# Edge lists in DRAM, read back in chunks, and other buffer depths in the edge-sum stage of a graph block

## Chip, cores and metric

The kernel runs on one core of a Trainium2 chip. The metric is the device time of one launch in microseconds (us), the median of three runs. The profile is of one further execution, with a span from its first to its last instruction.

## The reference

There are 6250 nodes with 256 features each and 200000 edges, sorted by target. In short:

```python
xn  = layernorm(x)
# graph part: weighted sum over neighbours, self loop included
deg = count of edges into a node + 1;  dinv = 1/sqrt(deg)
h   = xn @ gnn_W
g   = relu(segment_sum(h[src] * (dinv[src]*dinv[dst]), dst) + dinv^2*h + gnn_b)
# mixer: linear attention over all nodes, layer norm, two-layer MLP, layer norm
x   = x + g + mix(xn)
# feed-forward: each node goes to the best of 8 experts, capacity 977
x   = x + expert_ffn(layernorm(x))
```

## The kernel before

The nodes are 49 blocks of 128 (the last has 106). The program has three stages.

**Stage 1, to about 300 us.** It normalizes x, computes q, k and v, and searches the sorted list of targets for where each block begins (`search`). Scaled rows `xs = xn*dinv` go in two forms: as three bf16 parts in SBUF (`xs3`, 128 partitions x 49 blocks x 768) and as float32 pairs in DRAM (`g_dram`, 2 KB a row). `edge_lists` then writes four lists that stay in SBUF to the end of stage 2: `idx` and `rel` (for each of 816 tiles of 128 edges the source row and the target's place in its block) and `hiT` and `loT` (for each of 25 even blocks, 22 groups of 2 x 128 edges, the block and place of each source). At the end a flag is read; if the data does not fit the layout, a general path (`tc.If(flag == 1)`) computes the sums instead and empties the lists.

**Stage 2, about 302 to 1645 us.** It sums over the edges, in two ways, and does the rest of the graph part and of the mixer beside it. Three Python generators are interleaved by hand (`tc.manual_schedule`), so every engine has one fixed order:

- `gather`, for the 24 odd blocks, 34 tiles each, 816 in all. Step j starts the indirect DMA of 128 rows of `g_dram` into `gt` (L891, on POOL's queue), and builds a one-hot `oh` of the targets on DVE (L895). It then multiplies tile j - LAG: `ps += oh^T gt` (L906, 512 columns, in PSUM pool `gaps` with two banks). The first tile of a block is preceded by two matmuls with the identity (L903, L904) that add the self loop. The last is followed by `put_sum`: ACT copies one half of `ps` out (L825), DVE adds the other (L827). `GB` = 9 buffers hold `gt` and `oh`; `LAG` = 7.
- `dense`, for the 25 even blocks. A block takes 11 steps. A step builds four pairs of one-hots on DVE (`onehots`: `lo` 128 wide at L838, `hi` 294 wide at L840), multiplies the pairs of the step before (L874, four matmuls into two PSUM tiles `bp`, pool `bups` with two banks), and ACT casts both to a slice of the count matrix `A` (L875). Beside it, the matrix of the block before is multiplied with `xs3`: some 15 matmuls a step (L858) into `ps_d`, copied out by `put_sum`.
- `rounds`, 25 rounds of two blocks: the mixer for one pair, and for an earlier pair, whose sums are there, the graph weight, layer norm, gate, choice of expert, and an indirect DMA of its rows to `xbuf` (L984, also on POOL's queue).

The interleaving is set by counts: one step of `gather` in each pass of the loop, `dense` in proportion (286 steps on 823 passes, about one in three), and `SIDE` = 0.74 steps of `rounds`. PSUM's eight banks are spent as `mmps` 3 (for `rounds`), `gaps` 2, `deps` 1, `bups` 2.

**Stage 3, from about 1700 us.** The eight experts run one after the other from `xbuf`, and rows are scattered to the output.

Of the kernel before, what the change touches and what calls it, by code (L numbers as in the profile page):

```python
# [17 lines left out]
P = 128  # L18
N_NODES = 6250
N_EDGES = 200000  # L20
D = 256
# [22 lines left out]
EB = 34  # L44
NGT = NGB * EB
NGC = (NGT + P - 1) // P
GB = 9
LAG = 7
SIDE = 0.74
NX = 6  # L50
FIRST = 0.58
ROW = 2 * D + 2
# [10 lines left out]
def graph_block_kernel(  # L63
# [30 lines left out]
    g_dram = dram.tile([N_NODES, 2 * D], F32, name="g_dram")  # L94
    agg = dram.tile([AGR, D], F32, name="agg")
    deg_dram = dram.tile([AGR, 1], F32, name="deg_dram")
    q_dram = dram.tile([len(twos), P, 2, 2 * P], F32, name="q_dram")
    xbuf = dram.tile([SLOTS, ROW], F32, name="xbuf")

    main = ExitStack()  # L100
    lists = main.enter_context(tc.tile_pool(name="lists", bufs=1))
    idx = lists.tile([P, NGC * P], I32, name="idx")
    rel = lists.tile([P, NGC * P], F32, name="rel")
    hiT = lists.tile([P, NDC, 2, 5 * NG], F32, name="hiT")
    loT = lists.tile([P, NDC, 2, 5 * NG], F32, name="loT")
    big = main.enter_context(tc.tile_pool(name="big", bufs=1))
    xs3 = big.tile([P, NB, 3 * D], BF16, name="xs3")
    xv = xs3.bitcast(F32)
# [353 lines left out]
    def edge_lists():  # L462
# [55 lines left out]
        for c in range(NGC):  # L518
            if c % 4 == 0:
                et = [rps.tile([P, 512], F32, name="et_ps", tag="et_ps", bufs=2) for _ in range(2)]  # L520
            gd, gs = got.pop(c)
            gf, gf2 = gd.bitcast(F32), gs.bitcast(F32)
            V.tensor_scalar(gf, gd, nfirst[:, c:c + 1], None, op0=OP.subtract)
            V.tensor_copy(gf2, gs)
            yield
            for e, w in zip(et, (gf, gf2)):
                nc.tensor.transpose(e[:, c % 4 * P:(c % 4 + 1) * P], w, ident)
            ask(c + 2)
            yield
            if c % 4 == 3 or c == NGC - 1:  # L530
                for o, e in zip((rel, idx), et):
                    nc.scalar.copy(o[:, (c - c % 4) * P:(c + 1) * P], e[:, :(c % 4 + 1) * P])
                yield
        for c in range(NDC):
            wd, ws = got.pop(NGC + c)
# [14 lines left out]
            lf = hs.bitcast(F32)  # L550
            V.tensor_copy(lf[:W], ws[:W])
            yield
            for v, o in ((kf, hiT), (lf, loT)):
                et_ps = rps.tile([P, 512], F32, name="et_ps", tag="et_ps", bufs=2)
                for h in range(2):
                    nc.tensor.transpose(et_ps[:, h * W:(h + 1) * W], v[:W, h * P:(h + 1) * P], ident[:W, :W])
                nc.scalar.copy(o[:, c].rearrange("p h g -> p (h g)"), et_ps[:, :2 * W])
            ask(NGC + c + 2)
            yield
        V.scalar_tensor_tensor(vend[:W], first[:W], float(N_EDGES - 2 * P) - 0.5, vend[:W], op0=OP.is_lt, op1=OP.mult)  # L560
# [147 lines left out]
    with tc.If(flag == 1):  # L708
        with tc.tile_pool(name="gp", bufs=1, side="right") as gp:
# [91 lines left out]
            for t0, n in fours:  # L801
# [1 line left out]
                xs = slot4("xs").rearrange("p (t d) -> p t d", d=D)  # L803
                nc.sync.dma_start(xs[:r, :n, :], node_rows(agg, t0, n))
                all_of(in_parts(t0, n, xs))
            V.memset(rel, -1.0)
            V.memset(hiT, 400.0)
    early.close()


    with tc.tile_pool(name="ga", bufs=GB, side="right") as ga, \
            tc.tile_pool(name="de", bufs=2, side="right") as de, \
            tc.tile_pool(name="gaps", bufs=2, space=PSUM) as gps, \
            tc.tile_pool(name="deps", bufs=1, space=PSUM) as dps, \
            tc.tile_pool(name="bups", bufs=2, space=PSUM) as bps, \
            tc.manual_schedule():
        sums = {}
        there = set()
# [2 lines left out]
        def put_sum(t, ps):  # L821
            gi = t // 2
            if gi not in sums:
                sums[gi] = pair("G", 3, "ag")
            nc.scalar.copy(sums[gi][:, t % 2, :], ps[:, :D])  # L825
            if t % 2:
                V.tensor_tensor(sums[gi][:, 1, :], ps[:, D:], sums[gi][:, 1, :], op=OP.add)  # L827
            there.add(t)

        def onehots(u, p):  # L830

            c, b = divmod(u, 5)
            o = []
            for g in (2 * p, 2 * p + 1):
                for h in range(2):
                    col = b * NG + g
                    lo = de.tile([P, P], BF16, name="lo", tag="lo", bufs=8)
                    V.tensor_scalar(lo, rowb, loT[:, c, h, col:col + 1], None, op0=OP.is_equal)  # L838
                    hi = de.tile([P, NB * GN], BF16, name="hi", tag="hi", bufs=8)
                    V.tensor_scalar(hi, hib, hiT[:, c, h, col:col + 1], None, op0=OP.is_equal)  # L840
                    o.append((lo, hi))
            return o

        def dense():

            mats, made = {}, None
            acc_ps = None
            half = NG // 2
            for u in range(ND + 1):
                for p in range(half):  # L850
                    if u >= 1 and p >= 1:

                        A = mats[u - 1]
                        if p == 1:
                            acc_ps = dps.tile([P, D], F32, name="ps_d", tag="ps_d")
                        for hi in range((p - 1) * NB // (half - 1), p * NB // (half - 1)):
                            for h in range(3):
                                nc.tensor.matmul(acc_ps, A[:, hi, :], xs3[:, hi, h * D:(h + 1) * D],  # L858
                                                 start=(hi == 0 and h == 0), stop=(hi == NB - 1 and h == 2))
                    coming = None  # L860
                    if u < ND:
                        if p == 0:
                            mats[u] = de.tile([P, NB, P], BF16, name="A", tag="A")
                        coming = (u, p, onehots(u, p))
                    if made is not None:
                        uu, pp, oh = made
                        for i in range(2):
                            g = 2 * pp + i
                            w = GN if g < NG - 2 else 4
                            at = GN * g if g < NG - 1 else P - 4  # L870
                            bp = bps.tile([P, 512], F32, name="bp", tag="bp")
                            for h in range(2):
                                lo, hi = oh[2 * i + h]
                                nc.tensor.matmul(bp[:, :NB * GN], lo, hi, start=(h == 0), stop=(h == 1))  # L874
                            nc.scalar.copy(mats[uu][:, :, at:at + w],  # L875
                                           bp[:, :NB * GN].rearrange("p (s k) -> p s k", k=GN)[:, :, :w])
                        if pp == half - 1:

                            V.tensor_tensor(mats[uu][:, 2 * uu, :], mats[uu][:, 2 * uu, :], identb, op=OP.add)
                    made = coming  # L880
                    if u >= 1 and p == half - 1:
                        put_sum(2 * (u - 1), acc_ps)
                    yield

        def gather():
            tiles = {}
            ps = None
            for j in range(NGT + LAG):
                if j < NGT:
                    gt = ga.tile([P, 2 * D], FR, name="gt", tag="gt")  # L890
                    nc.gpsimd.indirect_dma_start(  # L891
                        out=gt, out_offset=None, in_=g_dram,
                        in_offset=bass.IndirectOffsetOnAxis(ap=idx[:, j:j + 1], axis=0))
                    oh = ga.tile([P, P], FR, name="oh", tag="oh")
                    V.tensor_scalar(oh, rowb, rel[:, j:j + 1], None, op0=OP.is_equal)  # L895
                    tiles[j] = (gt, oh)
                i = j - LAG
                if i >= 0:
                    k, e = divmod(i, EB)
                    t = 2 * k + 1  # L900
                    if e == 0:
                        ps = gps.tile([P, 2 * D], F32, name="ps", tag="ps")
                        nc.tensor.matmul(ps, identb, xs3[:, t, :2 * D], start=True, stop=False)  # L903
                        nc.tensor.matmul(ps[:, D:], identb, xs3[:, t, 2 * D:], start=False, stop=False)  # L904
                    gt, oh = tiles.pop(i)
                    nc.tensor.matmul(ps, oh, gt, start=False, stop=(e == EB - 1))  # L906
                    if e == EB - 1:
                        put_sum(t, ps)
                yield
# [266 lines left out]
                    lgt = None  # L1176

        G, Dn, S = gather(), dense(), rounds()
        n_dense = (ND + 1) * (NG // 2)
        done_d = done_s = 0  # L1180
        alive = {"g": True, "d": True, "s": True}

# [7 lines left out]
        j = 0  # L1190
        while any(alive.values()):
            step("g", G)
            while alive["d"] and done_d * (NGT + LAG) < n_dense * (j + 1):
                step("d", Dn)
                done_d += 1
            while alive["s"] and done_s < SIDE * (j + 1):
                step("s", S)
                done_s += 1
            j += 1
# [141 lines left out]
```

## Time and profile before

| what | value |
|---|---|
| runs | 2054.58, 2057.87, 2075.50 us; median 2057.87 |
| profiled execution, own time / span | 2051.43 / 2049.6 us |
| TensorE clock granted, mean | 0.905 |
| PE, DVE, ACT, POOL busy, whole span | 80%, 62%, 34%, 45% |
| stage 2, 302 to 1645 us: PE, DVE, ACT, POOL busy | 1097.3, 964.0, 407.8, 841.0 us of 1343 |
| stage 2: granted clock, share of DMA engines | 0.91, 0.70 |

PE stands for TensorE's matmuls, DVE for VectorE, ACT for ScalarE, POOL for GpSimd, SP for SyncE, which issues most plain DMAs. The busy time of PE counts modelled ends of pipelined matmuls. A wait is idle time of an engine, put down to what ended it.

### The profile page before, as it was taken

Reading aid. Unit: us, or ns where it says so; the run is one execution under the profiler, and the core shown is the slowest. Engines: PE = TensorE matmul, PEld = TensorE weight load, DVE = VectorE, ACT = ScalarE, POOL = GpSimd, SP = SyncE. Lnnn points to the kernel's source line nnn. Section 1 sums busy time; section 2 is a strip of 40 time slices with the busy share of each in tenths; the row PEclk is TensorE's granted clock in tenths of the full one; section 3 lists DMA queues with packets and bytes.
Section 4 is the critical chain, followed back from the end, with each engine's and each line's share of the span. In section 5 each row is a group of like instructions: output and inputs, shape, how many; then the busy total and the mean of one; then the engine's idle time right before and its main releaser. Section 6 shows DMA issues by size and latency. Waiting matters only on the chain. (4 is left out here: it accounts for less than half of the span.)

```text
span 2049.6 us, 28653 instructions
## 1 busy us (share of the span) xinstructions
PE 1648.4 (80%) x9171; PEld 1203.4 (59%) x9171; DVE 1275.3 (62%) x5337; ACT 700.4 (34%) x1627; POOL 924.3 (45%) x957
## 2 busy tenths in 40 slices
PE   5787866887888888887878787887878737999996
PEld 2454544666666666665656565665656525586774
DVE  5767657677767778686757677776867431232332
ACT  2657952233333333232323232332323112233332
POOL 1022006666666666656656666665665610011111
PEclk9888997999998989898989899898999958999998
DMA  7346767777776677767767676667676615414220
GB/s 214 100 133 196 253 182 194 181 183 196 184 187 173 182 182 189 194 161 193 187 180 180 183 181 169 171 185 183 171 179 170 172 35 188 174 49 146 99 96 19
DMA packets 211319, 337.83 MB, mean 165 GB/s; under 512 B 30047, under 2 KB 79002, under 8 KB 211018
## 3 DMA queue, kind: packets, MB, share of 16 engines
q0 software_dynamic: 125424, 232.93, 44.3%
q1 hardware_dynamic: 85434, 101.74, 15.5%
q8 instruction: 81, 1.33, 0.3%
q10 hardware_dynamic: 288, 1.08, 0.1%
q14 instruction: 92, 0.75, 0.1%
HBM read 278.29 MB, written 60.06 MB: 165 GB/s over the span
## 5 line engine op out<-in xcount | busy, mean ns | idle before, releaser
L891 POOL DMA_INDIRECT gt<-g_dram,idx x816 | 794.8, 974 | 576.1 <-issue 168.7
L858 PE MATMUL ps_d<-xs,A 128*128 128x256 bf16 x3675 | 489.4, 287 | 41.3 <-issue 37.5
L875 ACT CAST A<-bp 128x294 bf16<-128x294 f32 (+1 forms) x550 | 200.6, 401 | 832.8 <-PE bp L874 231.0
L858 PEld LDWEIGHTS <-A 128*128 128x128 bf16 x3675 | 355.5, 103 | 171.5 <-issue 112.9
L906 PE MATMUL ps<-gt,oh 128*128 128x512 f32 x816 | 335.1, 484 | 42.6 <-DMA gt<-g_dram,idx 32.3
L840 DVE TENSOR_SCALAR hi<-hib,hiT 128x294 bf16<-128x294 bf16 x1100 | 351.0, 323 | 1.1 <-issue 1.1
L874 PE MATMUL bp<-hi,lo 128*128 128x294 bf16 x1100 | 216.0, 305 | 120.2 <-ACT A L875 39.6
L838 DVE TENSOR_SCALAR lo<-rowb,loT 128x128 bf16<-128x128 bf16 x1100 | 269.9, 245 | 3.2 <-PE ps_d L858 1.2
L895 DVE TENSOR_SCALAR oh<-rowb,rel 128x128 fp32r<-128x128 bf16 x816 | 207.2, 288 | 76.2 <-remote 30.4
L874 PEld LDWEIGHTS <-lo 128*128 128x128 bf16 x1100 | 109.6, 102 | 180.9 <-issue 57.3
L906 PEld LDWEIGHTS ps<-gt,oh 128*128 128x128 f32 x816 | 153.3, 206 | 76.5 <-DMA gt<-g_dram,idx 37.4
L1285 POOL DMA_INDIRECT out<-rep,who x43 | 42.4, 986 | 314.7 <-DVE rep L1283 226.8
L1257 PE MATMUL hpf<-xet,w1e 128*128 128x512 f32 (+2 forms) x544 | 154.1, 441 | 8.7 <-ACTq L1297 3.5
L1267 PE MATMUL ypf<-w2e,hm 128*128 128x256 f32 (+1 forms) x688 | 151.3, 379 | 0.0
L1267 PEld LDWEIGHTS ypf<-w2e,hm 128*128 128x128 f32 (+1 forms) x688 | 128.9, 188 | 21.9 <-issue 3.1
L1257 PEld LDWEIGHTS hpf<-xet,w1e 128*128 128x128 f32 x544 | 86.5, 193 | 70.0 <-issue 62.9
L1269 DVE TENSOR_TENSOR y<-ypf,fb_s 128x256 f32<-128x256 f32 (+1 forms) x43 | 18.2, 423 | 138.8 <-PE ypf L1267 138.8
L662 PE MATMUL mm<-wqkv_s,xnt 128*128 128x512 f32 (+1 forms) x196 | 101.5, 644 | 0.0
L1259 ACT ACTIVATE hm<-hpf,fb_s 128x512 f32<-128x512 f32 (+2 forms) x136 | 70.9, 525 | 84.6 <-PE hpf L1257 81.2
L1051 DVE TENSOR_SCALAR z<-mm 128x8 f32<-128x8 f32 (+1 forms) x49 | 7.9, 162 | 138.6 <-remote 82.6
L984 POOL DMA_INDIRECT xbuf<-slot,put x49 | 51.8, 1058 | 74.5 <-issue 45.4
L1101 ACT ACTIVATE s<-s,nb,rs 128x256 f32<-128x256 f32 (+1 forms) x98 | 53.6, 599 | 47.3 <-DVE rs_sr L194 29.8
(289 smaller groups left out, 2034.1 us busy)
## 6 DMA issues: line engine op xcount, KB each, us to landing
gt<-g_dram,idx POOLq DMA_INDIRECT x816
g_dram<-two SPq DMA_DIRECT2D x24, 512.0 KB
xt<-in_x SPq DMA_DIRECT2D x42, 256.0 KB
xbuf<-zeros SPq DMA_DIRECT2D x26, 384.0 KB
xe<-xbuf SPq DMA_DIRECT2D x8, 1028.0 KB
w1e<-in_fw SPq DMA_DIRECT2D x8, 1024.0 KB
w2e<-in_fw SPq DMA_DIRECT2D x8, 1024.0 KB
xe<-xbuf SPq DMA_DIRECT2D x8, 771.0 KB
```

The source lines that it names most:

```text
L662: nc.tensor.matmul(kp[:r, :], xnt[:, c, i * r:i * r + r], wqkv_s[:, c, D:3 * D], start=(c == 0), stop=(c == 1))
L838: V.tensor_scalar(lo, rowb, loT[:, c, h, col:col + 1], None, op0=OP.is_equal)
L840: V.tensor_scalar(hi, hib, hiT[:, c, h, col:col + 1], None, op0=OP.is_equal)
L858: nc.tensor.matmul(acc_ps, A[:, hi, :], xs3[:, hi, h * D:(h + 1) * D], start=(hi == 0 and h == 0), stop=(hi == NB - 1 and h == 2))
L874: nc.tensor.matmul(bp[:, :NB * GN], lo, hi, start=(h == 0), stop=(h == 1))
L875: nc.scalar.copy(mats[uu][:, :, at:at + w], bp[:, :NB * GN].rearrange("p (s k) -> p s k", k=GN)[:, :, :w])
L891: nc.gpsimd.indirect_dma_start(out=gt, out_offset=None, in_=g_dram, in_offset=bass.IndirectOffsetOnAxis(ap=idx[:, j:j + 1], axis=0))
L895: V.tensor_scalar(oh, rowb, rel[:, j:j + 1], None, op0=OP.is_equal)
L906: nc.tensor.matmul(ps, oh, gt, start=False, stop=(e == EB - 1))
L1257: nc.tensor.matmul(hp[:, :nn], w1e[:, c, f * P:(f + 1) * P], xet[:, c, at:at + nn], start=(c == 0), stop=(c == 1))
L1259: nc.scalar.activation(hm[:, f, :nn], hp[:, :nn], AF.Relu, bias=fb1_s[:, e * 8 + f:e * 8 + f + 1])
L1267: nc.tensor.matmul(yp[:r, :], hm[:, f, (i - i0) * P:(i - i0) * P + r], w2e[:, f, :], start=(f == 0), stop=(f == DFF // P - 1))
```

## The change

1. The four lists are no longer SBUF tiles. In stage 1 ACT copies each piece into a staging tile `st` (two buffers), and an SP DMA stores it in DRAM (`idx_l`, `rel_l`, `hi_l`, `lo_l`): 4 stores for the first two lists, 10 for the others. In stage 2 `gather_lists(c)` reads 128 columns of `idx` and `rel`, `dense_lists(c)` 220 columns of `hiT` and `loT`, into a pool `chunks` with two buffers. Chunks 0 and 1 are read at the start of the stage, the others about half a chunk to more than a chunk ahead. The general path empties the lists in DRAM.
2. `dense` keeps the one-hots of two steps instead of one; `lo` and `hi` have 12 buffers instead of 8. The product with `xs3` and the casts follow two steps behind the one-hots.
3. `bups` has three banks instead of two, `gaps` one instead of two. Between two blocks `gather` now gives one pass of the loop to the others without doing anything itself.
4. `GB` is 11 instead of 9, `LAG` 9 instead of 7. `SIDE` is 0.72, since there are now 848 passes instead of 823.

The core of the diff:

```diff
-GB = 9
-LAG = 7
-SIDE = 0.74
+GB = 11
+LAG = 9
+SIDE = 0.72
...
-    idx = lists.tile([P, NGC * P], I32, name="idx")
-    rel = lists.tile([P, NGC * P], F32, name="rel")
-    hiT = lists.tile([P, NDC, 2, 5 * NG], F32, name="hiT")
-    loT = lists.tile([P, NDC, 2, 5 * NG], F32, name="loT")
+    idx_l = dram.tile([P, NGC * P], I32, name="idx_l")      # rel_l, hi_l, lo_l likewise
...
-                    nc.scalar.copy(o[:, (c - c % 4) * P:(c + 1) * P], e[:, :(c % 4 + 1) * P])
+                    st = rw.tile([P, 512], F32, name="st", tag="st")
+                    ...
+                    nc.scalar.copy(st, e[:, :(c % 4 + 1) * P])
+                    nc.sync.dma_start(o[:, (c - c % 4) * P:(c + 1) * P], st)
...
-            tc.tile_pool(name="gaps", bufs=2, space=PSUM) as gps, \
+            tc.tile_pool(name="gaps", bufs=1, space=PSUM) as gps, \
-            tc.tile_pool(name="bups", bufs=2, space=PSUM) as bps, \
+            tc.tile_pool(name="bups", bufs=3, space=PSUM) as bps, \
...
+        def part(name, source, dtype=F32):
+            t = chunks.tile([P, source.shape[-1]], dtype, name=name, tag=name)
+            nc.sync.dma_start(t, source)
+            return t
...
+        gather_lists(0)
+        dense_lists(0)
+        gather_lists(1)
+        dense_lists(1)
...
+            for n in range((ND + 1) * half + 2):
+                u, p = divmod(n, half)
+                if u < ND:
+                    ...
+                    made.append((u, p, onehots(u, p)))
+                m = n - 2
+                ...                 # product of block u-1, counts and casts of step m
...
                     if e == 0:
+                        if k:
+                            yield
                         ps = gps.tile([P, 2 * D], F32, name="ps", tag="ps")
```

## The prediction

> **What bounds the kernel now.** I began with the page's busy times by slices, to see where the change lands.
>
> ```profile
> PE   5787866887888888887878787887878737999996
> ...
> POOL 1022006666666666656656666665665610011111
> PEclk9888997999998989898989899898999958999998
> ```
>
> Slices 7 to 32 are the edge sums (stage 2): PE near eight tenths, POOL near six, a granted clock that flickers below full. In the last slices PE is at nine and the clock at full, so the low clock belongs to a PE that stops and starts. The first and last stages are hardly touched; the forecast is about stage 2. Its sum by engine:
>
> ```profile
> 302.00:1645.00 1343.00, 1097.28 (x6925) 827.60 (x6924) 964.02 (x4391) 407.76 (x970) 841.04 (x860) 0.91 0.70 181
> ```
>
> PE 82%, DVE 72%, ACT 30%, POOL 63%, DMA 70%: no engine is full. POOL is fuller than it looks:
>
> ```profile
> L891 POOL DMA_INDIRECT gt<-g_dram,idx x816 | 794.8, 974 | 576.1 <-issue 168.7
> ```
>
> In the timeline, gathers in a row start 1.24 to 1.28 us apart: 0.94 to 0.97 busy and a constant 0.30 between. 816 x (0.974 + 0.30) = 1040 us, and 49 scatters to xbuf of 1.058 + 0.30 add 67: POOL alone needs 1106 of the 1343 us. PE's 1097 holds cold time; DVE needs 964. Three engines of similar load, each in a fixed order, lose the rest to each other. So next I read what PE waits for in this stage:
>
> ```profile
> PE bp L874 <- ACT A L875: 39.6, 26, 3.3
> PE ps_d L858 <- issue: 37.5, 49, 2.2
> PE ps L906 <- DMA gt<-g_dram,idx: 32.3, 24, 2.7
> PE bp L874 <- DVE lo L838: 17.0, 12, 8.5
> PE bp L874 <- issue: 16.5, 26, 3.2
> PE bp L874 <- DVE hi L840: 14.7, 14, 2.1
> ```
>
> All PE waits there come to some 240 us: for the bp banks 40, for one-hots or for other DVE work queued in front of them about 52 (17.0 + 14.7 and twelve smaller rows), for gathers 32 and 10 more before L906 with no cause shown, for nothing shown elsewhere about 70, for the mixer's own chains the rest. The last view is the timeline at a change of gathered block:
>
> ```profile
> 858.23 0.39 PE L903 MATMUL ps<-xs,identb 128*128 128x512 bf16 x1
> ...
> 861.74 0.71 ACT L875 CAST A<-bp 128x294 bf16<-128x294 f32 x2 [5.93 <-remote]
> 862.07 0.94 POOL L891 DMA_INDIRECT gt<-g_dram,idx  x1 [1.61 <-remote]
> 862.19 1.14 PE L874 MATMUL bp<-hi,lo 128*128 128x294 bf16 x4 [2.99 <-ACT A L875]
> ...
> 862.59 0.41 ACT L825 COPY ag<-ps 128x256 f32<-128x256 f32 x1
> ...
> 863.03 0.42 DVE L827 TENSOR_TENSOR ag<-ps,ag 128x256 f32<-128x256 f32 x1 [4.06 <-ACT ag L825]
> ```
>
> Two things are to be seen. The next block's first matmul (L903) runs 5.2 us before the old bank is empty (863.45), which needs the second gaps bank. And ACT and POOL are let go together, long after the matmuls that they wait for are shown.
>
> **What the Trainium skill says.** "TensorE: Matmul & The Clock Gate", section on the HAM clock gate, says that an idle PE falls to half clock and is full again after about 3.4 us of sustained work. The trace agrees in kind: 0.97 busy goes with clock 1.00 in the last stage, 0.82 with 0.91 here. A mean of 0.91 between half and full means 18% of the time at half. "Perfetto Trace Analysis", section on TensorE instructions, says that a matmul's shown end is an estimate; so part of PE's "wait for ACT" may be work, and I discount it. "DMA: Bandwidth & Descriptors", anatomy of one DMA, gives about 2 us fixed per DMA, which I use for the first chunk reads. Gathers here take longer: those started at 304.64 and 305.96 let their matmuls go at 310.00 and 311.41, 5.4 us.
>
> **Part by part.** The sum is made against the profiled execution, 2051.4 us by its own time; the median of the runs shown, 2057.9, is 6.5 above it.
>
> *One-hots two steps ahead.* The same DVE instructions, 2200 of them, only earlier. DVE may still not run more than a step past PE (12 buffers hold three steps, as 8 held two), but PE may now run ahead of DVE by two steps before it stops. A step is 1343/286 = 4.7 us. The DVE rows are waits of 1 to 4 us (one of 8.5 at the start), so one more step covers nearly all; I keep the start and a few others, 14 us: -38. DVE's own stops for PE's results (113 us before z L1051 with "remote" and bp as releasers) are what fills this slack.
>
> *Three bp banks.* A step uses two. Before, the first bp of a step waits for the first cast of the step before; now that first bp finds a bank free and the second waits for the same cast. The gain per stop is one bp of two matmuls, 0.2 to 0.4 us, sometimes the whole of a short stop: 26 x 0.4 = -10. The 40 us do not go.
>
> *LAG 9, GB 11.* Gathers 9 ahead at 1.27 us each stand 11.4 us before use instead of 8.9, against 5.4 us of flight. The stops for gathers average 1.35 us and reach 2.7, and they follow the xbuf scatters: at 699.5 to 702.7 POOL stands still for a scatter's slot and then four scatters of 1.36 us alternate with gathers. Two more gathers in hand cover 2.5 us of each of these 12 places: of 42 us, -25. POOL must have had the time to run ahead; its waits for PE (141 us for L906 alone) say so.
>
> *Follow-on.* These are -73 together. With PE faster, POOL's 1.27 us per gather and the late releases (in 79 of 275 steps the cast is released by "remote" or by the later ps_d matmuls) become the next wait. I let a third come back there: -49. Fewer stops raise the granted clock; one point of 0.91 on 1097 us: -10 (0 to -30).
>
> *One gaps bank.* Now L903 waits for ACT's L825 and DVE's L827, and everything behind it on PE waits too: the counts, the dense product, the mixer. I measured in the timeline, at all 23 block changes, the end of L827 minus the start of L903: from -1.9 to 7.35 us, the positive ones 44.1 in sum. The added pass gives PE about 1.3 us of other work in between (1343/823 = 1.63 us a pass at PE's 82%); what stays above 1.3 sums to 24.1. The largest (7.35, 5.2, 5.1) lie where PE is stopping anyway, so some of it is not new: +20, between +5 and +44. Before this change this wait is absent; that is its full price.
>
> *Chunk reads.* 8 SP DMAs at the start, then 5 x 2 and 3 x 2 more, 64 gathers (105 us) or more than two blocks ahead; SP stands up to 62 us before an output store (L1089), but that store is earlier in the order, so the read is not late. The first idx chunk stands before the first gather and the first oh: DVE restarts at 299.94 after the flag, and a DMA needs 2 to 4 us after SP has passed it: +4 (2 to 8). The order behind SP's queue: the reads of xt and q for the first rounds, a few tenths of a us each, which have slack.
>
> *Stage 1.* ACT's copies are the same, 14 in number; 14 stores join SP's queue, each behind ACT's copy, with g_dram stores, xbuf blanks and xt loads behind them. xt is loaded three groups ahead. +2 (0 to 6). The freed list space costs nothing. The tail after 1645 is the same chain, with a two-gather shorter starve at its front, in the -25.
>
> Sum: -49 - 10 + 20 + 4 + 2 = -33, so 2018 for the profiled kind of execution; with the 6.5 us to the median, 2025. Rounded down a little, since PE's best stretches (19.4 of 20 us busy at full clock near 750 us) show how much room there is: 2022.
>
> **Rivals.** *More is freed.* If PE's stops feed each other through the clock, the -73 comes whole and the clock rises by three points: -73 - 30 + 26 = -77, about 1980; at most twice that, since POOL's 1106 and the stops that stay bound the stage near 1200. For it: windows with no scatter and no DVE burst run at clock 1.00. Against: the 79 late releases, which no buffer here removes.
>
> *Nothing moves.* PE's waits are partly not waits (modelled ends), and POOL with its 0.82 load sets the pace, as it does after each batch of scatters. Then -73 shrinks to -25, and the costs of 26 cancel it: about 2058.
>
> *Slower: the single gaps bank.* If the added pass carries no PE work (two passes of three have no dense step), each block change costs its measured gap, 44 us, and PE standing still there holds back the release of gathers too, so that POOL, at 1.27 us each, cannot catch up: 44 + 12 for POOL + 6 - 25 = +37, about 2095. It decides from a mean stop at L903 of about 3 us (23 x 3 = 69 against 73 gained, with the clock against the 6 of reads). Measured is 1.9 without any slack, so a doubling is needed.
>
> *The change does not do what it says* only in the banks: three banks for two tiles a step is half a step. That is in the -10.
>
> **How the numbers follow.** Forecast (2000 to 2037) 0.42; more is freed 0.18; nothing moves 0.18; the slow rival 0.22. A measurement of this kernel can tell about 1% from no change. Faster by over 1%: 0.60; within 1%: 0.18; slower: 0.22. Range: from 1955 (most of the second case) to 2092 (most of the last).
>
> **What would show it.** Right: the PE rows "bp <- DVE" fall from about 52 to under 20 us and "L906 <- DMA gt" under 20; a new row before L903 with ACT ag or DVE ag as its releaser, 10 to 30 us; "bp <- ACT A" still there; the granted clock in the stage at 0.92 or above; the first gather later by 2 to 8 us. Wrong: L903's row over 60 us, POOL back to back throughout with PE waiting for gt, or a longer first stage.

## The result, and the profile after

The changed kernel takes 2081.5 us (median of 16 runs, 2071.8 to 2089.2) beside 2058.1 us for the kernel before (16 runs): ratio 1.0115, 95% interval 1.0097 to 1.0134. It is slower by 23 us where 36 us faster was forecast. Later groups of runs fell on different chips, and these come in two kinds. On some the kernel before takes 2056 to 2068 us (kind S; the result above, and three more groups), on others 1878 us (kind F; two groups). Each ratio below is against runs of the kernel before in its own group; it can differ by up to 0.2% from the quotient of the two medians that stand beside it. On kind F the same change is *faster*, 0.9839 (0.9812 to 0.9867).

The profiled execution after took 2084.1 us, span 2082.3, clock 0.894 (before: 2051.4, 2049.6, 0.905). The same views as those shown of before; first the page's slices, and its row of the gathers:

```profile
PE   5787856778796978797878888887778746899996
...
POOL 1022016555665665655666666666566610111111
PEclk9799987999898988798999999898889867999998
...
L931 POOL DMA_INDIRECT gt<-g_dram,idx x816 | 794.6, 974 | 592.8 <-PE ps L948 167.5
```

Stage 2 now reaches to about 1680 us. The gathers cost POOL the same (974 ns each), but the first starts at 302.26 and the last at 1669.32, one in 1.677 us; before it was 302.10 to 1640.94, one in 1.643. 28 of the 33 us between the two profiled executions are there. The stage's sum by engine, over a window that holds all of it:

```profile
302.00:1680.00 1378.00, 1096.10 (x6929) 828.86 (x6929) 968.82 (x4398) 405.01 (x971) 840.66 (x860) 0.89 0.69 178
```

No engine does noticeably more than before (PE 1097, DVE 964, POOL 841): the stage has become longer by idle time. PE's waits in it, after:

```profile
PE ps_d L901 <- issue: 50.1, 69, 1.9
PE bp L912 <- ACT A L913: 40.7, 26, 7.7
PE ps L945 <- DVE ag L838: 31.6, 12, 7.6
PE mm L208 <- ACT ag L836: 24.8, 6, 6.9
PE ps L948 <- DMA gt<-g_dram,idx: 18.9, 13, 4.2
PE mm L1087 <- DMA q<-q_dram: 17.8, 1, 17.8
...
PE bp L912 <- DVE hi L874: 5.3, 4, 3.0
```

Four of the six signs that the prediction named are there: all of "bp <- DVE" fell from 47 to 13 us (the 52 of the prediction is all of PE's waits for DVE, 5 of them not at bp), the gathers' row from 32 to 19, the row of the single gaps bank (L945) appeared, with 32 just above the range, and "bp <- ACT" stayed at 41. Two are not: the clock in the stage is 0.89 and not 0.92, and the first gather is 0.16 us late and not 2 to 8. And the waits of the stage sum to 288 us, before to 240. I put the rows of both kernels together by what waits: bp for DVE -34, gathers for DMA -13, but the identity matmuls for DVE +36, the mixer's matmuls for ACT +32 (24 to 55), ps_d without a cause +13, the first rounds' matmul for its q +18. What was taken away at one matmul is paid, by these rows, at others.

The chunk reads show at the start of the stage. The first gather is only 0.16 us late, but xt and q of the first rounds now stand behind eight list reads on SP, which before had gone ahead of the branch at the end of stage 1:

```profile
299.35 0.37 SPq L843 DMA_DIRECT2D idx<-idx_l  x1
...
310.35 1.22 PE L1087 MATMUL mm<-kvb,q 128*128 128x132 f32 x4 [17.82 <-DMA q<-q_dram]
```

This matmul started at 302.83 before, and the first product of a gather at 305.58; now that is 314.07. The first list read started at 299.35 and let the first gather go at 302.26, 2.9 us later. (The 2 us that the prediction took for such a read are, in the section of the Trainium skill that it names, those of DMAs issued by GpSimd; these are SP's.)

Last, a stretch of the timeline in the middle of the stage, which turned out to be the most telling (PE's, ACT's and POOL's lines):

```profile
854.42 2.14 PE L901 MATMUL ps_d<-xs,A 128*128 128x256 bf16 x9
855.15 0.94 POOL L931 DMA_INDIRECT gt<-g_dram,idx  x1 [0.31 <-PE ps L948]
...
858.33 0.37 PE L901 MATMUL ps_d<-xs,A 128*128 128x256 bf16 x1 [1.77 <-issue]
...
859.76 0.37 PE L901 MATMUL ps_d<-xs,A 128*128 128x256 bf16 x1 [1.06 <-issue]
860.59 0.94 POOL L931 DMA_INDIRECT gt<-g_dram,idx  x1 [0.30 <-issue]
861.17 0.37 PE L901 MATMUL ps_d<-xs,A 128*128 128x256 bf16 x1 [1.03 <-issue]
863.27 0.37 PE L901 MATMUL ps_d<-xs,A 128*128 128x256 bf16 x1 [1.73 <-issue]
...
864.22 0.71 ACT L913 CAST A<-bp 128x294 bf16<-128x294 f32 x2 [16.78 <-remote]
864.37 1.19 PE L912 MATMUL bp<-hi,lo 128*128 128x294 bf16 x4
864.55 0.94 POOL L931 DMA_INDIRECT gt<-g_dram,idx  x1 [3.03 <-remote]
```

Dense matmuls, which have all their operands and elsewhere run 15 in 1.81 us, creep along one at a time, over a microsecond apart and without a semaphore to wait for, while POOL issues gathers one after the other; the count matmuls that ACT casts here had been shown at 849.37. Then POOL runs out of free buffers and stops (861.53), and three microseconds later everything is let go at once. The prediction had seen these late releases ("let go together, long after the matmuls that they wait for are shown") and given them a third of the gain.

### The profile page after: what moved, and what is told of

Its sections match the earlier page's. It is cut to its first block, busy times and chain, and to the rows that moved or that the text cites. A ratio compares the mean times of both kernels' runs of the same rounds, so it can differ in the third digit from the quotient of the medians.

```text
span 2082.3 us, 28761 instructions
## 1 busy us (share of the span) xinstructions
PE 1643.0 (79%) x9171; PEld 1203.0 (58%) x9171; DVE 1277.9 (61%) x5337; ACT 697.5 (33%) x1627; POOL 924.2 (44%) x957
## 3 DMA queue, kind: packets, MB, share of 16 engines
q0 software_dynamic: 125424, 232.93, 43.8%
## 5 line engine op out<-in xcount | busy, mean ns | idle before, releaser
L901 PE MATMUL ps_d<-xs,A 128*128 128x256 bf16 x3675 | 499.1, 289 | 52.9 <-issue 50.1
L948 PE MATMUL ps<-gt,oh 128*128 128x512 f32 x816 | 329.8, 479 | 26.8 <-DMA gt<-g_dram,idx 18.9
L912 PE MATMUL bp<-hi,lo 128*128 128x294 bf16 x1100 | 208.9, 307 | 72.0 <-ACT A L913 40.7
```

## The experiments

Theory A is the prediction's ledger: a relieved wait is time, less a third. Theory B: something else paces stage 2, and a relieved wait reappears elsewhere. In the first group A also says that the loss is the single gaps bank; B is called a rival there, and a theory C says that the loss is the late start of the stage.

### First group, kind S (before 2067.8 us): which part costs

**The change with the old banks**, and without the extra pass between two blocks.

```diff
-SIDE = 0.72
+SIDE = 0.74
-            tc.tile_pool(name="gaps", bufs=1, space=PSUM) as gps, \
+            tc.tile_pool(name="gaps", bufs=2, space=PSUM) as gps, \
-            tc.tile_pool(name="bups", bufs=3, space=PSUM) as bps, \
+            tc.tile_pool(name="bups", bufs=2, space=PSUM) as bps, \
-                        if k:
-                            yield
-        n_gather = NGT + LAG + NGB - 1
+        n_gather = NGT + LAG
```

> The changed kernel with the old split of PSUM banks: two for the gathered sums, two for the counts, no empty pass between blocks (825 passes, SIDE 0.74). Lists in DRAM, one-hots two steps ahead and LAG 9 stay. Theory A (the single gaps bank is the loss): the 32 us of PE waiting at L945 for DVE and the waits of the mixer's transposes that follow from it go, time 2040 to 2050. Rival B (DVE's lateness is only met at another place, since PE has one order): the waits come back at the counts or the mixer, time 2070 to 2085. Rival C (the late start of the stage is the loss): 2070 to 2080.

Measured: 2068.2 us, ratio 1.001 (0.9994 to 1.0025): the loss is gone, but the 2040 to 2050 that theory A expected are missed.

**Before, with only the bank swap** and its extra pass: the same edit the other way round, in the kernel before.

```diff
-            tc.tile_pool(name="gaps", bufs=2, space=PSUM) as gps, \
+            tc.tile_pool(name="gaps", bufs=1, space=PSUM) as gps, \
-            tc.tile_pool(name="bups", bufs=2, space=PSUM) as bps, \
+            tc.tile_pool(name="bups", bufs=3, space=PSUM) as bps, \
```

> The kernel before with only the banks moved: one for the gathered sums with an empty pass between blocks (848 passes counting as in the changed kernel, SIDE 0.72), three for the counts. Theory A: 2078 to 2100, a row of 25 to 45 us of PE waiting for DVE ag before the identity matmuls. Rivals B and C: within 8 us of 2058.

Measured: 2080.2 us, 1.0077 (1.0055 to 1.0098). PE's waits show where:

```profile
PE ps L905 <- DVE ag L827: 19.7, 8, 5.5
```

**Lists in DRAM alone**: the edit of the first run, and `dense` and the two depths as before.

```diff
-GB = 11
-LAG = 9
+GB = 9
+LAG = 7
-            mats, made = {}, []
+            mats, made = {}, None
...
-                    lo = de.tile([P, P], BF16, name="lo", tag="lo", bufs=12)
+                    lo = de.tile([P, P], BF16, name="lo", tag="lo", bufs=8)
```

> The kernel before with only the lists moved to DRAM and read back in chunks; banks 2 and 2, one step ahead, GB 9, LAG 7, SIDE 0.74. Theory C: eight list reads stand on SP's queue after the flag, ahead of the first reads of x and q, which before were issued ahead of the flag; the first matmul of the mixer comes some 9 us later and the whole is 2066 to 2074. Theory A: within 5 us of 2058.

Measured: 2069.4 us, 1.0004 (0.9989 to 1.002). The start is late here too: the first product of a gather comes at 316.13.

**The change with the first xt and q reads ahead of the branch** (they are what the first `next(S)` issues), and four list reads at the start instead of eight.

```diff
-        gather_lists(0)
-        dense_lists(0)
-        gather_lists(1)
-        dense_lists(1)
-            if b == 2 and p == 0 and c:
+            if b == 2 and p == 0:
-                    if w == P // 2 and c:
+                    if w == P // 2:
...
-        done_d = done_s = 0
+        next(S)
+        gather_lists(0)
+        dense_lists(0)
+        done_d, done_s = 0, 1
```

> The changed kernel with the first reads of x and q put ahead of the list reads in the order (and with that ahead of the flag), and chunk 1 of the lists read half a chunk later, so that four list reads instead of eight stand at the start. Theory C: 8 to 12 us less than the changed kernel, about 2071. Theory A: same as the changed kernel to 5 us, or the gain is taken up later by the waits in the stage.

Measured: 2099.2 us, 1.0155 (1.0138 to 1.0172). The first product of a gather came at 310.12 instead of 314.07, and the whole, each against the kernel before in its own group, became 0.4% (some 8 us) slower than the change instead of faster. Why is open: the edit also moves a step of `rounds` and the later list reads in the order. Theory C has no support from it.

What follows: the swap of banks costs 0.77% (16 us, between 11 and 20) alone and 1.05% (22 us) inside the change, which is all of the loss; given the noise the two prices can't be told apart. It was run as a whole, with its extra pass and its `SIDE`; neither these nor the third bp bank were run by themselves. The lists in DRAM cost nothing that can be measured, late start included. And the two parts that were to bring 63 us bring nothing: 1.001 with them, 1.0004 without.

### Second group, same chip as the first (before 2068.0): the two parts by themselves, and what sets the pace

**One-hots two ahead only**, with lists in DRAM, old banks, LAG 7, GB 9. Against the lists alone:

```diff
-            mats, made = {}, None
+            mats, made = {}, []
...
-                    lo = de.tile([P, P], BF16, name="lo", tag="lo", bufs=8)
+                    lo = de.tile([P, P], BF16, name="lo", tag="lo", bufs=12)
```

> Edit lists in DRAM as after, banks of before (two for gathered sums, two for counts), 7 gathers ahead as before, and of the change only the one-hots built two steps ahead. The same without the two-ahead measured 1.0004 of before. Theory A (the prediction's): a stop of PE for a one-hot is lost time, so -38 us, a third given back: ratio 0.985 to 0.99. Theory B (PE's one order: a stop that goes reappears at the next matmul, because another engine sets the pace): 0.997 to 1.003, with bp<-DVE down from 63 us to under 30 and the total of PE's waits unchanged.

Measured: 2067.2 us, 1.0007 (0.9986 to 1.0028). "bp <- DVE" is 22 us in its trace against 63 without the edit, the sum of PE's waits 271 against 279.

**LAG 9 and GB 11 only**, with lists in DRAM and old banks, one-hots one ahead. Against the lists alone:

```diff
-GB = 9
-LAG = 7
+GB = 11
+LAG = 9
```

> Lists in DRAM and the banks of before, one-hots one step ahead, and of the change only LAG 9 and GB 11 (two more gathers in flight). Theory A: -25 us less a third, ratio about 0.992. Theory B: 0.997 to 1.003. A third possibility is a loss: every block's sum is complete two passes later in PE's order while the mixer's rounds keep their place, 1.003 to 1.008.

Measured: 2068.6 us, 1.0018 (1.0 to 1.0035). PE's row of waits for gathers is 8 us in its trace against 21 without the edit.

**Half the gathers**, in the change with the old banks:

```diff
-                    gt = ga.tile([P, 2 * D], FR, name="gt", tag="gt")
-                    nc.gpsimd.indirect_dma_start(
+                    if j % 2 == 0:
+                        gt = ga.tile([P, 2 * D], FR, name="gt", tag="gt")
+                        nc.gpsimd.indirect_dma_start(
```

> After with the banks of before, and only every second tile's rows gathered: the odd tile's matmul reads the rows of the tile before it, so half of the computation's gathered rows are left out. PE, ACT and DVE do the same work; POOL loses 408 gathers of 1.27 us (518 of its 1106 us) and the DMA half its bytes. If POOL's issue or the gathers' landing sets the pace of the stage (a form of the rival 'nothing moves'), the time falls by 60 us or more, ratio under 0.97. If PE's order with the late releases of ACT and DVE sets it, the fall is 25 us at most (the waits for gt), ratio 0.985 to 1.0.

Measured: 1826.0 us, 0.8827 (0.8793 to 0.8861): 242 us less, though PE waited for gathers only 22 us by its own row in the kernel with all of them. ACT's waits for the counts, first with all gathers and old banks (first run of the first group), then with half:

```profile
ACT A L913 <- remote: 342.5, 59, 18.0
ACT A L913 <- PE bp L912: 206.5, 119, 7.3
ACT A L913 <- PE ps L946: 146.3, 76, 9.6
ACT A L913 <- PE ps_d L901: 111.0, 23, 7.7
```

```profile
ACT A L913 <- PE bp L912: 427.5, 196, 9.3
...
ACT A L913 <- PE ps L947: 72.7, 36, 6.4
ACT A L913 <- remote: 54.3, 11, 11.1
```

The late releases ("remote", where the matmul that was waited for had long been shown) go with the gathers, 342 to 54 us. POOL's instructions and the bytes are not all that changes in this run: 11 buffers of `gt` now hold the rows for 22 tiles, so POOL may run much further ahead of PE.

**Half the wide one-hots**:

```diff
-                    hi = de.tile([P, NB * GN], BF16, name="hi", tag="hi", bufs=12)
-                    V.tensor_scalar(hi, hib, hiT[:, col:col + 1], None, op0=OP.is_equal)
+                    if h == 0:
+                        hi = de.tile([P, NB * GN], BF16, name="hi", tag="hi", bufs=12)
+                        V.tensor_scalar(hi, hib, hiT[:, col:col + 1], None, op0=OP.is_equal)
```

> After with the banks of before, and the second wide one-hot of each count left out: its matmul uses the first one's, so the counts are not those of the second half. PE, ACT and POOL do the same work; DVE loses 550 instructions of 0.32 us, 176 of 970 us in the stage. If DVE's load sets the pace (directly, or because the mixer's steps, the block sums' additions and the gather one-hots stand behind the one-hots in its queue), ratio 0.97 or less. If not, 0.99 to 1.0.

Measured: 2062.5 us, 0.9973 (0.9956 to 0.999). DVE with 176 us less work moves the time by 5.5: it does not set the pace.

What follows: theory B holds on this chip. Either part does to its own row what was forecast and nothing to the time that can be told from noise.

### Third group, a chip of kind F (before 1877.6 us): bytes, coupling, PE

**Half of each row** (1 KB), in the change with the old banks:

```diff
-                    gt = ga.tile([P, 2 * D], FR, name="gt", tag="gt")
+                    gt = ga.tile([P, D], FR, name="gt", tag="gt")
-                        out=gt, out_offset=None, in_=g_dram,
+                        out=gt, out_offset=None, in_=g_dram.rearrange("n (c d) -> (n c) d", c=2),
-                    nc.tensor.matmul(ps, oh, gt, start=False, stop=(e == EB - 1))
+                    nc.tensor.matmul(ps.rearrange("p (c d) -> p c d", c=2), oh,
+                                     gt.unsqueeze(1).to_broadcast([P, 2, D]), start=False, stop=(e == EB - 1))
```

> After with the banks of before, and every gather fetches only the first half of each row (1 KB instead of 2 KB): the matmul reads that half twice, so the second half of each gathered row is left out. POOL issues the same 816 gathers of 128 rows, PE, DVE and ACT do the same work; only the bytes are halved. Leaving out every second gather brought 242 us. If that came from POOL's issue (1.27 us a gather, 1106 us of the stage), this run changes little: ratio 0.98 to 1.0. If it came from the bytes that the DMA engines move, it brings most of the 242 us: ratio under 0.93.

Measured: 1837.2 us, 0.9795 (0.9765 to 0.9825). POOL's row in the groups of instructions (busy us, mean ns of one, then idle before them and what ended it) is what it is with whole rows on such a chip (987 ns in the next group):

```profile
L931 POOL DMA_INDIRECT gt<-g_dram,idx x816 | 801.9, 983 | 369.1 <-issue 123.1 <-DMA rel<-rel_l 116.5 <-PE ps L946 59.3
```

**GB 11 with LAG 7** in the change with the old banks:

```diff
-LAG = 9
+LAG = 7
```

> After with the banks of before and LAG 7 in place of 9, GB stays 11. In the kernel before and in the change GB minus LAG is 2: a gather and its one-hot need the buffer of the matmul that the order puts two passes earlier, so POOL and VectorE can't get more than two passes ahead of PE. Here it is four. If this coupling is what loses the time that no engine needs (stage 1343 us against POOL 1106 and PE 1097), ratio 0.96 to 0.985. If the gathers' own rate or landing is the limit, 0.995 to 1.005, and PE waits for gt again.

Measured: 1869.3 us, 0.9964 (0.9948 to 0.9981).

**Two of the three parts of the dense product**, in the change with the old banks:

```diff
-                        for h in range(3):
+                        for h in range(2):
...
-                                             start=(hi == 0 and h == 0), stop=(hi == NB - 1 and h == 2))
+                                             start=(hi == 0 and h == 0), stop=(hi == NB - 1 and h == 1))
```

> After with the banks of before, and the dense product with two of its three parts (h = 2 is left out): PE loses 1225 matmuls of 0.13 us at full clock, about 160 us of its 1088 busy us as profiled; POOL, DVE, ACT and the gathers stay. If PE's own order and load set the pace, ratio 0.93 to 0.95. If the gathers set it, 0.985 to 1.0, and PE's stops grow by what its work shrinks.

Measured: 1838.0 us, 0.9814 (0.9783 to 0.9845). PE had 1225 matmuls less to do, yet between 302 and 1470 us its busy time fell by 86 us only, from 1027.7 (the same kernel with all three parts, next group) to 942.1, as its clock fell from 0.94 to 0.91. Its row of waits for gathers, 65 us with all three parts, says where the rest went:

```profile
PE ps L946 <- DMA gt<-g_dram,idx: 133.6, 140, 3.4
```

What these three mean shows only beside the change itself on such a chip, in the next group.

### Fourth group, another chip of kind F (before 1878.3 us): the change there

Four kernels from above: the change unaltered, the change with the old banks, that with half rows, and that with LAG 7.

> The changed kernel unaltered, beside the kernel before on the chip of this group. The group before this one ran on a chip where the kernel before takes 1877.6 us instead of 2058 to 2068, with POOL issuing nearly without a pause. If the loss comes from the gaps bank alone, it is there on either kind of chip: 1.007 to 1.015 on a slow one; on a fast one, where PE waits for gathers anyway, part of each stop at a block change is absorbed by gathers that land meanwhile: 1.002 to 1.012. If the more gathers in flight pay where gathers are the limit, after is at or below 1.0 on a fast chip.

The change: 1849.3 us, 0.9839 (0.9812 to 0.9867).

> After with the banks of before (two for gathered sums, two for counts). On a slow chip it repeats 1.001. On a fast one: 0.99 to 1.0 if two more gathers in flight or the earlier one-hots pay there, 1.0 to 1.005 if they don't. Its distance from the unaltered change in the same group is the price of the bank swap: 1.0 per cent on the slow chip; the same on the fast one if it is PE's standing still that costs, less if gathers set the pace.

With the old banks: 1845.9 us, 0.9824 (0.9795 to 0.9854).

> Half of each gathered row left out (1 KB instead of 2 KB, read twice by the matmul), all else as after with the banks of before. On the fast chip 0.9795 of before. If this group's chip is slow: leaving out every second gather brought a ratio of 0.883 there. If the bytes are what that chip is slow in, under 0.93; if it is the number of gathers (POOL's instructions and what each of them makes the other engines wait for), 0.98 to 1.0.

Half rows: 1835.5 us, 0.9771 (0.9734 to 0.9807).

> GB 11 with LAG 7, banks of before, one-hots two ahead, lists in DRAM. On the fast chip 0.9964 of before. On a slow one, if the distance of two passes between a buffer's release and its next gather is what loses time there: 0.97 to 0.99; if not, 0.998 to 1.003. Beside the run with LAG 9 in the same group it shows what the two passes are worth.

LAG 7 instead of 9: 1869.3 us, 0.9946 (0.9928 to 0.9965).

So on kind F the change brings 29 us, by its medians: 23 of them from LAG 9 instead of 7, 9 from the lists, the earlier one-hots and GB 11 together, and -3 from the bank swap, which can't be told from nothing there. PE's waits in the unaltered change on this chip, to the stage's end at about 1460 us:

```profile
PE ps L948 <- DMA gt<-g_dram,idx: 55.4, 62, 3.1
PE mm L208 <- ACT s L1143: 24.2, 24, 5.6
PE ps L945 <- DVE ag L838: 19.9, 10, 5.9
PE mm L1087 <- DMA q<-q_dram: 17.2, 1, 17.2
```

then the page's slices of the same run, and the first row of ACT's waits:

```profile
PE   4787884898898989898989898998998459999996
...
POOL 0104003777777777776777777777777201101111
PEclk9888997899999999998999999999999779999998
```

```profile
ACT A L913 <- PE bp L912: 604.5, 235, 7.7
```

ACT waits only for counts that are really not there; no "remote" row is left, no ps_d without a cause. POOL stands at seven tenths instead of six, PE's clock at nine. The first and last gather start at 304.55 and 1440.49: one in 1.394 us; with the old banks 305.77 and 1434.17, 1128 us for what POOL alone needs 1106 for by the prediction's sum. By these figures POOL's issue is the pace here; the run that would test it, half of the gathers, is missing on kind F. That also reads the third group: PE's 1225 matmuls (0.9814 without them, 0.9824 with) are worth next to nothing, half of the bytes about 10 us (1835.5 against 1845.9), hardly more than the noise.

The wait at L945 is still 20 us, but half of it replaces waits for gathers: their row is 55 us here and 65 with the old banks, and the sum of all PE's waits in the stage is 143.7 us in both.

What LAG 9 removes is not mainly the wait for gathers. With LAG 7 the row is 64 us, with LAG 9 65; but with LAG 7 PE also waits at the same matmul behind other work of DVE:

```profile
PE ps L946 <- DMA gt<-g_dram,idx: 63.9, 56, 4.2
...
PE ps L946 <- DVE hi L874: 14.6, 10, 3.6
PE ps L946 <- DVE lo L872: 6.8, 7, 2.0
```

All such rows together are 34 us with LAG 7 and 2.4 with LAG 9: a gather's one-hot `oh` stands in DVE's queue in the pass of its gather, so two more passes are two more passes for DVE to be late in. That is read from the rows; no run moved the one-hot alone. GB minus LAG, four here and two in the kernel before, is worth at most the 9 us above: as the coupling that loses the stage's idle time it was to bring 1.5 to 4%.

### Fifth group, a third chip, kind S (before 2056.3 us)

**LAG 9 and GB 11 with one-hots one ahead** (the second group's kernel):

> Lists in DRAM, the banks of before, one-hots one step ahead, LAG 9 and GB 11. On the slow chip 1.0018. On a fast one, the same with one-hots two ahead is 0.9824, and with LAG 7 and two ahead 0.9946. If the two more gathers ahead are the whole gain there, as PE's only large wait is for gathers: 0.98 to 0.986. If the one-hots two ahead give what the prediction gave them (38 us, a third handed back): 0.992 to 1.0.

Measured: 2051.6 us, 0.9986 (0.9969 to 1.0003).

**One more of each**:

```diff
-GB = 11
-LAG = 9
+GB = 12
+LAG = 10
```

> The same with one more: LAG 10 and GB 12, which the one-step one-hots leave room for. If gathers that wait for use are what a fast chip lacks, a further 3 to 10 us below the run with LAG 9: 0.977 to 0.983 there, and the fastest of all that compute the whole; if POOL's issue of 1.25 us a gather is already reached, the same as LAG 9 within 0.003. On a slow chip 0.998 to 1.004.

Measured: 2067.2 us, 1.0054 (1.0034 to 1.0074).

**Half the gathers**:

> Every second gather left out (the odd tiles' matmuls read the rows of the tile before). On the slow chip this took 1826 us, 242 less than before there. If what makes the slow chip slow is tied to the gathers (about 190 us for 816 of them), a fast chip runs this kernel in nearly the same time, 1800 to 1840 us: ratio 0.96 to 0.98. If the chips differ in something else, it keeps its distance of 190 us: about 1640 us, ratio 0.87 to 0.89.

Measured: 1814.7 us, 0.882 (0.8789 to 0.8852).

On kind S, then, two more gathers in flight gain at most a fraction of a per cent, and a third one loses 0.7% against them, for a reason that is open; the 242 us that half of the gathers cost repeat on a second chip of the kind (241.6). Whether the one-hots two ahead matter on kind F was to be seen here and was not, since the chip was of the other kind; and the half of the gathers on kind F was not run.

No version beat both kernels on both kinds. The change with the old banks comes nearest: 1.001 and 0.9824.

## Why the prediction was wrong

| step | forecast, us | kind S | kind F |
|---|---|---|---|
| one-hots two ahead | -38 | 0 (1.0004 to 1.0007) | at most -9, with lists and GB 11 |
| LAG 9, GB 11 | -25 | +4 and -3 (1.0018, 0.9986), not told from 0 | -23 (LAG alone) |
| three bp banks and one gaps bank | -10 and +20 | +16 to +22 | +3, not told from 0 |
| lists: reads and stage 1 | +6 | 0 (1.0004) | in the -9 |
| a third comes back | +24 | all of it comes back | - |
| clock | -10 | lower than before (0.894 against 0.905) | - |
| sum, measured whole | -33 | +23 | -29 |

**The step that failed** is "Follow-on: I let a third come back there". On chips of kind S, as that of the result, all of the 63 us of the one-hots and gathers came back: the ratios are 1.0007 and 1.0018 with one of the two and 1.001 with both, beside 1.0004 with neither. The prediction had read the right sign for it, the late releases, and then gave "a third" without a working. The runs show what it is worth: the waits at bp and at the gathers did fall as counted, and the mixer's waits for ACT and the causeless ps_d took their place. The rival "nothing moves" had this part right, though not its reason: POOL did not issue steadily. It stopped again and again for buffers that PE had to free, and took 1.64 us a gather against 1.27.

**The bank swap** is the second. Its bounds (+5 to +44) held, its value did not: +20 for the gaps bank less 10 for the third bp bank was to leave +10, and 16 to 22 was measured, 36 us of wait at the identity matmuls. What the third bp bank is worth was not measured: all of "bp <- ACT" fell from 44 to 36 us with the swap alone, about the 10 that the prediction counted, but a fallen row was not time in the other two parts either. The slow rival had the place and the mechanism, a single gaps bank that holds up everything behind L945; its other half, that POOL can't catch up, fits the 1.677 us a gather but was not tested. Its sign of a stop of 3 us at every change did not come: 13 stops, 36 us in all, are 1.5 us over the 23 changes.

**Chunk reads.** The prediction said that xt and q "have slack". They had none: PE's first attention product stands 17.8 us for q. The price at the end of the kernel was nevertheless nothing, +4 forecast; the lists-only run shows it.

**The clock** in the stage was to rise from 0.91 to 0.92 and fell to 0.89, with PE busy for 1096 of 1378 us (80%) instead of 82%. On kind F it is 0.95 in the stage, with PE busy for 1023 of 1158 us (88%). So the traces agree in kind with what the prediction took from the section on the HAM clock gate of "TensorE: Matmul & The Clock Gate" in the Trainium skill, that an idle PE falls to half clock (their clock records hold only full and half); the direction of PE's idle time is what the prediction had wrong.

**LAG** came out at 23 of the 25 us on kind F, which is luck: the forecast was made from the waits of a chip of kind S, where it brings nothing, and the rows of kind F point to VectorE's one-hot and not to the gather's flight. The 5.4 us of flight were also a long case: the very first gather before let its product start after 3.5 us (302.10 to 305.58), and where the trace of the change on kind F lets a gather be followed to its landing (510 of 816) the median is 3.8 us.

What stays open: why PE's news comes late on kind S, and whether it is the news or PE's matmuls themselves that are late. That it is tied to the gathers is shown (342 to 54 us of "remote" with half of them, on one chip; 63 us in all ACT's rows on another); whether to POOL's issuing, to the transfers or to the buffers of `gt` is not, since the half rows and the LAG 7 with more buffers ran on kind F only.

## What to carry to other kernels

Before a wait is credited with its length, look for rows in which an engine is let go late with no cause that the profile can name: while such rows hold a stage, buffers and look-ahead only move the waits, and a run that halves the suspect's work tells more than the sum of the rows. A bank that the end of one accumulation and the start of the next share can cost its drain at every change: 16 to 22 us for 23 changes where PE waits little for gathers (19 us), nothing that can be told where it waits for them anyway (55 us). One chip's ratio is one chip's: this change is 1.2% slower on one kind and 1.6% faster on another.

## What the runs showed of the hardware

- The same kernel takes 2056 to 2068 us on chips of kind S and 1878 on two others, 9% less, with the same work, the same 1.24 to 1.25 us from gather to gather where POOL runs freely, and the same gather row (974 to 989 ns).
- One difference in the trace is how PE's completions are recorded. Between 400 and 1500 us the trace's records of the semaphore that PE counts up number 1647 in the profile after of the result, and 755 of them follow another within 60 ns, mostly at 34 ns; 68 silences are over 4 us. In the change on kind F, 2082 are recorded, none closer than 60 ns, and 7 silences are over 4 us. With half the gathers on kind S it is 235 of 1961, and 24. "Perfetto Trace Analysis" of the Trainium skill, section on TensorE instructions, says that a matmul's shown end is an estimate, and its summary of the profiler's windows that the passing on of its semaphore is not in them; the silences may be what this hides.
- The records themselves differ too. In the same stretch of the profile after, 1827 of PE's instructions count a semaphore up and 1647 counts are recorded; of DVE's 2604 only 1369 are, of ACT's 760 only 446. On kind F hardly one is missing (2082 of 2084, 3006 of 3006, 860 of 860). So a wait on kind S that the profile puts down to nothing ("issue") can be one whose record is missing; a "remote" row rests on a record that is there.
- The transfers are not slower on kind S. In the change the packets of POOL's queue filled 43.8% of the 16 DMA engines' 2082.3 us there and 48.9% of their 1849.4 us on kind F: 912 and 904 us.
- In "Perfetto Trace Analysis" of the Trainium skill, section on the DMA instruction of GpSimd, the shown end is that of writing the descriptors, not of the transfer. The runs agree: 989 ns a gather with 1 KB rows, 987 with 2 KB, on one chip of kind F.
